# The first third of a turn: where two layer norms stand on VectorE and ScalarE

## The chip, the cores and the metric

The kernel runs on one core of one Trainium2 chip. The metric is the device time of that core in microseconds. Five engines work at once, each through its own instructions in order: TensorE (PE: products, and PEld: its weight loads), VectorE (DVE), ScalarE (ACT), GpSimd (POOL) and SyncE (SP), which here issues transfers. They wait for each other by semaphores.

## The reference, cut to what matters

The input is `x`, 64 graphs of 256 nodes with 256 features, and `adj`, 64 matrices of 256x256 with zeros and ones. Two layers follow each other, all in float32.

```python
# layer 0
h = _gat(x, adj, W1, a1);  h = _gat(h, adj, W2, a2)     # two graph attentions
h = _layernorm(x + h, g_ln1, b_ln1)                     # norm 0 in the kernel
ff = relu(h @ w_ff1 + b_ff1) @ w_ff2 + b_ff2
x = _layernorm(h + ff, g_ln2, b_ln2)                    # norm 1
# layer 1 (8 heads of 32)
scores = q @ k.T / sqrt(32);  attn = softmax(scores)
out = sum over r < 4 of (attn * (adj == r)) @ v_r
x = _ln(x + out @ Wo + bo, g1, beta1)                   # norm 2
ff = gelu(x @ W1 + b1) @ W2 + b2
return _ln(x + ff, g2, beta2)                           # norm 3
```

A norm is `(x - m) * rsqrt(v + eps) * g + b` with mean `m` and variance `v` over the 256 features of a node. With zeros and ones in `adj`, only two of the four values of `r` occur. A second path for other inputs is in the program; it doesn't run here.

## The kernel before, in words

**Groups and turns.** Two graphs make a group: 512 nodes, four blocks of 128. There are 32 groups, and the main loop calls `turn(y_, x_, z)` for u = 0 to 31 with three groups in three phases: `Y` (group u) goes through the attention and the hidden layer of layer 1, `X` (group u+1) through norm 0, the hidden layer of layer 0 and norm 1, and `Z` (group u+2) through the graph attentions. In turn 31 there is no `X`, in turns 30 and 31 no `Z`. The last norm (norm 3) of group u isn't done in its own turn: the turn puts `(y_, y)` on the list `waiting`, and the next turn does the norm in its first third. So turns 1 to 30 hold a waiting last norm and the first norm of `X`; turn 0 holds the first norm alone, turn 31 neither. The last two groups store their result piece by piece in another way.

**Order.** Inside `turn`, `tc.manual_schedule` makes the order of the text the order of TensorE, SP, VectorE and ScalarE (of TensorE and SP alone when there is no `X`). GpSimd's order is left to a scheduler.

**Products of seven.** The matrix products are done with seven products of quarters instead of eight. Their steps have numbers: `p("q1 v1 q2")` issues steps 1 of the query and key product (`q`), 1 of the value product (`v`) and 2 of `q`, each two matmuls in the source, four records in the trace. Two PSUM banks each collect them: steps 1, 6, 7, 4 go to one, steps 2, 5, 3 to the other. After 2, 5, 3 and 4 ScalarE copies the bank out (L1034), after 2, 6 and 7 VectorE adds (L1038). The next step into the same bank waits for that: v5 for the copy after v2, q7 for the sum after q6. The hidden layers do the same with `first("2a 1a 5a")`: a and b are two halves, ScalarE copies `h1b` (L905) after 2, 5 and 3, VectorE adds `h1a` (L908) after 1, 6 and 7.

**A norm** has these pieces. `moments`: one BN_STATS (L826) and one aggregation (L827) per block on VectorE. `norm`: the moments, then GpSimd's `rs = (v + eps) ** -0.5` (L837, L838). `applied_norm`: VectorE's offset `nm = -m * rs` (L846), then per block ScalarE's `y * rs + nm` (L853). The scale and shift of the last norm follow much later in the turn.

**The first third of a turn** in the order of the text: the four differences for the seven products (`p.sums()`); q1 v1 q2; norm 0 of `X` applied to blocks 0 and 1; the statistics of the waiting last norm, all four blocks; v2 q5; norm 0 applied to blocks 2 and 3, then `normed_features`, which transposes the four blocks on VectorE (L694) into `yt` and moves them into `hT` by 12 transfers on SP (L713) and four copies on GpSimd (L711); the scores of the first of four head groups (`sp`, L1082) and their exponentials (L1091), in two halves between v5, q3 and v3; the adjacency masks (`ea`, L1095); the waiting last norm applied, four blocks; the rest of the seven products; the sums over nodes (`es`, L1100). Then `first_hidden` forms four differences of `hT` (`tt`, L879), scores, masks and sums of the second head group follow, the early transpose of `Z`'s features (`xT`, L1137), and the hidden layer of `X` is dealt between the attention products: 2a 1a 5a, the scores of head group 2, the product with head group 1, 3a 6a, 2b 1b, and so on.

Of the kernel before, what the change touches and what calls it, by code (L numbers as in the profile page):

```python
# [12 lines left out]
ALU = mybir.AluOpType  # L13
# [372 lines left out]
def narrow_path(  # L386
# [13 lines left out]
    nc = tc.nc  # L400
# [6 lines left out]
    NB = N // P  # L407
# [281 lines left out]
    def normed_features(u, l, xn, natural=False, queues=(nc.sync,)):  # L689


        yt = work.tile([P, Q, KB, T, 32], F32, tag="yt", name=f"yt{u}_{l}", bufs=1)
        for t in range(T):
            mark["transposed"] = nc.vector.transpose(  # L694
                yt[:, :, :, t].rearrange("p q k r -> p k q r"),
                xn[:, t].rearrange("p (k q c) -> p k q c", k=KB, c=32))
        if natural:
            hT = work.tile([P, KB, TN], F32, tag="hT", name=f"hT{u}_{l}")
            to = hT.rearrange("c k (t a r) -> c (k t) a r", a=Q, r=32)
            for q in reversed(range(Q)):  # L700
                for a in range(Q):
                    move = nc.gpsimd.tensor_copy if q == a else nc.sync.dma_start
                    move(to[q * 32:(q + 1) * 32, :, a], yt[a * 32:(a + 1) * 32, q].rearrange("c k t r -> c (k t) r"))  # L703
            return with_ones([hT[:, k] for k in range(KB)])
        hT = work.tile([P, Q, KB, T, 32], F32, tag="hT", name=f"hT{u}_{l}")
        n = 0
        for q in range(Q):
            for a in range(Q):
                to, at = hT[q * 32:(q + 1) * 32, a], yt[a * 32:(a + 1) * 32, q]
                if q == a:  # L710
                    nc.gpsimd.tensor_copy(to, at)  # L711
                else:
                    mark["placed"] = queues[n % len(queues)].dma_start(to, at)  # L713
                    n += 1
        return [hT[:, :, k].rearrange("p a t r -> p t a r") for k in range(KB)]
# [100 lines left out]
    def normed(u, l, y, blocks=range(T)):  # L816

        applied_norm(y, *norm(u, l, y, blocks))

    def moments(u, l, y, blocks, mv=None):  # L820
        n = f"{u}_{l}_{blocks[0]}"
        st = work.tile([P, T, 6], F32, tag="st", name=f"st{n}", bufs=1)
        if mv is None:
            mv = work.tile([P, T, 2], F32, tag="mv", name=f"mv{n}")
        for t in blocks:
            nc.vector.bn_stats(st[:, t, :], y[:, t, :])  # L826
            nc.vector.bn_aggr(mv[:, t, :], st[:, t, :])  # L827
        return mv

    def norm(u, l, y, blocks=range(T), mv=None):  # L830

        n, t0 = f"{u}_{l}_{blocks[0]}", blocks[0]
        bt = slice(t0, t0 + len(blocks))
        mv = moments(u, l, y, blocks if mv is None else blocks[len(blocks) // 2:], mv)
        rs = work.tile([P, T], F32, tag="rs", name=f"rs{n}")
        nm = work.tile([P, T], F32, tag="nm", name=f"nm{n}")
        nc.gpsimd.tensor_scalar(rs[:, bt], mv[:, bt, 1], EPS, 0.0, op0=ALU.add, op1=ALU.add)  # L837
        nc.gpsimd.tensor_tensor(rs[:, bt], rs[:, bt], mhalf[:, bt], ALU.pow)  # L838
        if l == 3:
            nc.gpsimd.tensor_add(high[:, bt], high[:, bt], mv[:, bt, 0])  # L840
        return blocks, mv, rs, nm

    def applied_norm(y, blocks, mv, rs, nm, part=None, gpsimd=False):
        bt = slice(blocks[0], blocks[0] + len(blocks))
        if part is None or part[0] == blocks[0]:
            nc.vector.scalar_tensor_tensor(nm[:, bt], mv[:, bt, 0], -1.0, rs[:, bt],  # L846
                                           op0=ALU.mult, op1=ALU.mult)
        for t in part or blocks:
            if gpsimd:
                nc.gpsimd.tensor_scalar(y[:, t, :], y[:, t, :], rs[:, t:t + 1], nm[:, t:t + 1],  # L850
                                        op0=ALU.mult, op1=ALU.add)
                continue
            mark["normed"] = nc.scalar.activation(y[:, t, :], y[:, t, :], AF.Identity,  # L853
                                                  bias=nm[:, t:t + 1], scale=rs[:, t:t + 1])
# [145 lines left out]
    def out_sums(u, l):  # L1000
        two = [work.tile([P, HPB, NB * N], F32, tag=t, name=f"{t}q{u}_{l}") for t in ("e", "ea")]
        return [t[:, :, i * N:(i + 1) * N] for t in two for i in range(2)]
# [90 lines left out]
    def masked(b, m, ab, e, ea, pairs=(0, 2)):  # L1093
        for a in pairs:
            nc.vector.tensor_tensor(ea[:, a:a + 2, :], e[:, a:a + 2, :],  # L1095
                                    ab[:, None, :].to_broadcast([P, 2, NB * N]), ALU.mult)
# [112 lines left out]
    def first_hidden(x_):  # L1209

        X = g[x_]
        hT = X["hT"]
        if x_ == 0:
            hT = [h.rearrange("p (t a r) -> p t a r", t=T, r=32) for h in hT]
        X["h1"] = work.tile([P, FB, TN], F32, tag="h1", name=f"h1{x_}_0", bufs=1)
        tt = work.tile([P, Q, KB, T, 32], F32, tag="yt", name=f"tt{x_}_0", bufs=1)
        return hidden_seven(x_, 0, hT, wf1s, bf1, AF.Relu, X,
                            tt.rearrange("p q k t r -> p (q k t r)"))

    def piece():  # L1220
        if left:
            next(left[0], None)

    def turn(y_, x_, z):
        Y, X, Z = (g.get(u) for u in (y_, x_, z))
        hT, y = Y["hT"], Y["y"]
        quads = [(b, m) for b in range(G) for m in range(KB)]
        p = Projections(y_, hT)
# [5 lines left out]
        def scores(n, heads=range(HPB)):  # L1234
            pe[n], e[n] = weighted(y_, *quads[n], q, k_, Y["aT"])
            powers(n, heads)

        def powers(n, heads):
            exps(pe[n], *e[n], heads)

        def masks(n, *pairs):
            masked(*e[n], *pairs)

        def totals(n):
            e[n] = node_sums(*e[n])

        def sums(n):
            b, m = quads[n]
            if m == 0:
                acc[b] = [psum.tile([P, 512], F32, tag=t_, name=f"{t_}{y_}_{b}") for t_ in ("po", "zo")]  # L1250
            applied(b, m, v, *e.pop(n), *acc[b])
# [8 lines left out]
        def first(names, ends=0):  # L1260

            if X:
                steps(names)
            else:
                for _ in range(ends):
                    piece()
# [3 lines left out]
                                            ("PE", "SP", "DVE", "Activation")[:4 if X else 2]})  # L1270
        with order:
            p.sums()
            p("q1 v1 q2")
            if X:
                applied_norm(X["y"], *X["n"], [0, 1])
            last = norm(waiting[0][0], 3, waiting[0][1]) if waiting else None
            p("v2 q5")
            if X:
                applied_norm(X["y"], *X.pop("n"), [2, 3])
                X["hT"] = normed_features(x_, 0, X["y"])  # L1280
            scores(0, ())
            p("v5")
# [1 line left out]
            if z + 1 < NG:  # L1284
                load_x(z + 1)
            p("q3 v3")
            masks(0, (0,))
            powers(0, (2, 3))
            if waiting:
                applied_norm(waiting[0][1], *last)  # L1290
            p("q6 v6 q7 v7")
            masks(0, (2,))
            totals(0)
            p("q4 v4")
            steps = first_hidden(x_) if X else None
            scores(1)
            masks(1)
# [1 line left out]
            if Z:  # L1299
                early(z)  # L1300
            sums(0)
            first("2a 1a 5a", 1)
            scores(2)
            sums(1)
            if X:
# [32 lines left out]
            if Z:  # L1338
                mv = moments(y_, 2, y, range(NB))
            else:  # L1340
                n = norm(y_, 2, y, range(NB))
# [13 lines left out]
            if Z:  # L1355
                n = norm(y_, 2, y, mv=mv)
            else:
                applied_norm(y, *n)
                n = norm(y_, 2, y, range(NB, T))
# [41 lines left out]
            if X:  # L1401
                n = moments(x_, 1, X["y"], range(NB))
# [6 lines left out]
            if X:  # L1409
                out.add(4)  # L1410
                n = norm(x_, 1, X["y"], mv=n)
            h1 = Y["h1"] = work.tile([P, FB, TN], F32, tag="h1", name=f"h1{y_}_1", bufs=1)
            second("2a 1a 2b 1b")
            second("5a 5b")
            if X:
                applied_norm(X["y"], *n, [0])
            if Z:
                affine(y, rg3, rb3)
# [51 lines left out]
    waiting = []  # L1470

    with tc.manual_schedule(engines={mybir.EngineType.PE, mybir.EngineType.SP}):
# [24 lines left out]
        first = HiddenOut(0, 0, g[0]["y"], g[0]["h1"], wf2s, out_sums(0, 0))  # L1497
# [9 lines left out]
        for u in range(NG):  # L1507
            turn(u, u + 1, u + 2)
# [16 lines left out]
@with_exitstack  # L1525
def tile_gat_layer__then__relational_attention_layer(ctx: ExitStack, tc: tile.TileContext, *args):
    nc = tc.nc
    keep = ctx.enter_context(tc.tile_pool(name="keep", bufs=1))
    bad = keep.tile([1, 1], I32, name="bad")
    narrow_path(tc, *args, bad)  # L1530
    with tc.If(nc.values_load(bad[0:1, 0:1], min_val=0, max_val=P) > 0):
        general_path(tc, *args)
# [30 lines left out]
```

## Time and profile before

| what | us |
|---|---|
| median of three runs | 3070.12 (3069.05 to 3071.68) |
| the profiled execution | 3069.44 |
| its span in the trace | 3067.8 |
| TensorE busy | 3003.6 (98%) |
| VectorE busy | 2624.0 (86%) |
| ScalarE busy | 1684.2 (55%) |
| GpSimd busy | 678.4 (22%) |

The granted clock of TensorE was 0.995 of full speed. A line of a timeline gives the start in us, the time, the engine, the line of the kernel, the operation, what it writes and reads, the shape, how many records are merged in it, and in brackets the idle time of the engine ahead of it and what ended that. For merged records the time is that of the whole row.

### The profile page before, as it was taken

How to read it: one execution, taken by the hardware profiler on the slowest of the kernel's cores; microseconds unless marked ns; L12 is line 12 of the kernel's file. 1: busy time of each engine (PE TensorE's matmuls, PEld its weight loads, DVE VectorE, ACT ScalarE, POOL GpSimd, SP SyncE). 2: the span in 40 equal slices, each digit the busy share in tenths (PEclk: the TensorE clock that was granted, in tenths of full speed). 3: DMA queues.
4: the chain of work that ended last, by engine and by line, in shares of the span. 5: the costliest groups of instructions: out<-in, count | busy, mean ns of one | idle time of the engine just before them, and what ended most of it. 6: DMA issues, size and time to landing. Idle time of an engine off the chain costs nothing.

```text
span 3067.8 us, 58503 instructions
## 1 busy us (share of the span) xinstructions
PE 3003.6 (98%) x22192; PEld 2460.3 (80%) x22192; DVE 2624.0 (86%) x5025; ACT 1684.2 (55%) x3404; POOL 678.4 (22%) x930
## 2 busy tenths in 40 slices
PE   7999999999999999999999999999999999999997
PEld 5788877888887888787887778887878887878876
DVE  4788888888888889888888888888888888888886
ACT  4455555655645555555555455556555555555553
POOL 4222121222211221221222112222112212122211
PEclk8999999999999999999999999999999999999999
DMA  5011111211111211111111112111112111121000
GB/s 146 13 35 35 38 36 25 44 37 39 35 35 32 44 37 39 32 29 40 40 36 36 39 25 44 37 39 34 36 32 44 36 39 33 25 44 37 18 13 16
DMA packets 428403, 113.25 MB, mean 37 GB/s; under 512 B 364586, under 2 KB 427604, under 8 KB 428116
## 3 DMA queue, kind: packets, MB, share of 16 engines
q1 hardware_dynamic: 418076, 102.20, 15.2%
q10 hardware_dynamic: 8984, 6.19, 0.8%
q8 instruction: 178, 2.92, 0.4%
q0 software_dynamic: 1056, 1.05, 0.1%
q14 instruction: 109, 0.89, 0.1%
HBM read 56.78 MB, written 16.78 MB: 24 GB/s over the span
## 4 chain that ended last, share of the span: by engine, by line
PE 85%; DVE 9%; ACT 2%; issue 2%; DMA 1%; SPq 1%; POOL 1%; DVEq 0%; POOLq 0%; ACTq 0%
PE yf L985 22%; PE h1a L896 15%; PE h1b L896 11%; PE po L1110 7%; PE qk L1051 5%; PE v L1051 5%; PE xpp L740 4%; PE yop L811 4%; PE ygp L811 3%; PE sp L1082 3%; PE hpp L800 2%; PE zo L1113 2%; DVE s L775 2%; DVE yt L694 1%; DVE eaq L971 1%
## 5 line engine op out<-in xcount | busy, mean ns | idle before, releaser
L905 ACT COPY h<-h1b 128x512 f32<-128x512 f32 x384 | 224.2, 584 | 393.8 <-PE h1b L896 389.3
L908 DVE TENSOR_TENSOR h<-h1a,h 128x512 f32<-128x512 f32 x384 | 262.7, 685 | 111.9 <-PE h1a L896 106.2
L1095 DVE TENSOR_TENSOR ea<-e,aT 128x1024 f32<-128x1024 f32 x256 | 306.4, 1218 | 21.6 <-ACT e L1091 21.6
L853 ACT ACTIVATE y<-y,nm,rs 128x256 f32<-128x256 f32 x450 | 243.8, 607 | 140.1 <-DVE nm L846 135.8
L1091 ACT ACTIVATE e<-sp 128x512 f32<-128x512 f32 x512 | 269.4, 608 | 43.7 <-PE sp L1082 40.4
L1123 POOL TENSOR_TENSOR low<-low,rq 128x16 f32<-128x16 f32 x64 | 13.9, 217 | 1043.4 <-DVE rq L1122 1043.4
L1034 ACT COPY qk<-qk 128x512 f32<-128x512 f32 x128 | 75.3, 589 | 286.9 <-PE qk L1051 286.9
L711 POOL COPY hT<-yt 32x256 f32<-32x256 f32 x244 | 207.7, 851 | 68.4 <-DVE yt L694 60.8
L826 DVE BATCH_NORM_STATS2 st<-y 128x6 f32<-128x256 f32 x512 | 207.6, 407 | 4.5
L993 DVE TENSOR_TENSOR y<-yf,y 128x256 f32<-128x256 f32 x448 | 182.9, 408 | 29.5 <-PE yf L985 29.4
L837 POOL TENSOR_SCALAR rs<-mv 128x4 f32<-128x4 f32 (+1 forms) x134 | 33.1, 247 | 750.7 <-DVE mv L827 744.9
L865 DVE TENSOR_TENSOR y<-y,rb 128x1024 f32<-128x1024 f32 (+1 forms) x130 | 166.8, 1283 | 3.2
L939 ACT ACTIVATE h<-h,cols 128x512 f32<-128x512 f32 x256 | 167.0, 713 | 1.5 <-DVE h L908 1.1
L862 DVE TENSOR_TENSOR y<-y,rg 128x1024 f32<-128x1024 f32 (+1 forms) x130 | 161.6, 1243 | 1.2 <-ACT y L853 1.1
L1100 DVE TENSOR_TENSOR es<-e 128x1024 f32<-128x1024 f32 x128 | 155.6, 1216 | 0.0
L703 POOL COPY hT<-yt 32x256 f32<-32x256 f32 x120 | 114.8, 957 | 169.4 <-DVE yt L694 165.2
L838 POOL TENSOR_TENSOR rs<-rs,mhalf 128x4 f32<-128x4 f32 (+1 forms) x134 | 146.6, 1094 | 8.4
L1082 PE MATMUL sp<-qk 32*128 32x256 f32 x2048 | 146.6, 400 | 0.1
L742 ACT COPY xp<-xpp 128x260 f32<-128x260 f32 x128 | 45.4, 386 | 171.5 <-PE xpp L740 171.4
L1038 DVE TENSOR_TENSOR qk<-qk,qk 128x512 f32<-128x512 f32 x96 | 65.9, 686 | 83.9 <-ACT qk L1034 65.1
L1110 PE MATMUL po<-e,v 128*32 128x256 f32 x2048 | 136.3, 384 | 0.0
L896 PE MATMUL h1a<-tt,wf 128*128 128x256 f32 x512 | 134.2, 386 | 0.3 <-DVE h L908 0.3
(280 smaller groups left out, 7645.5 us busy)
## 6 DMA issues: line engine op xcount, KB each, us to landing
hT<-yt SPq DMA_DIRECT2D x912, 32.0 KB, 1.9
y<-in_x_dram SPq DMA_DIRECT2D x32, 512.0 KB, 4.5
xq<-in_x_dram SPq DMA_DIRECT2D x240, 64.0 KB, 2.2
aq<-in_adj_dram SPq DMA_DIRECT2D x240, 64.0 KB, 2.4
out_dram<-y SPq DMA_DIRECT2D x30, 512.0 KB, 2.9
hT<-yt ACTq DMA_DIRECT2D x180, 32.0 KB, 1.9
wf<-in_L_gnn_w_ff_dram SPq DMA_DIRECT2D x2, 1024.0 KB, 7.3
w<-in_L_gnn_W_dram SPq DMA_DIRECT2D x2, 1024.0 KB, 7.7
```

The lines of the kernel that those rows point to most:

```text
L711: nc.gpsimd.tensor_copy(to, at)
L811: nc.tensor.matmul(ps[:, i * F:(i + 1) * F], lhs(t, k), rhs(b, k), start=(k == 0), stop=(k == n - 1))
L853: mark["normed"] = nc.scalar.activation(y[:, t, :], y[:, t, :], AF.Identity, bias=nm[:, t:t + 1], scale=rs[:, t:t + 1])
L896: nc.tensor.matmul(ps[:, i * N:(i + 1) * N], w_[:, f * P:(f + 1) * P], m, start=first and i == 0, stop=True, skip_group_check=True)
L905: mark["copied"] = nc.scalar.copy(out(h, o, b), pair(ps))
L908: mark["added"] = nc.vector.tensor_tensor(out(h, o, b), pair(one[h]), out(h, o, b), ALU.add)
L985: nc.tensor.matmul(s.ps[n][:, i * F2:(i + 1) * F2], a[:, k, i * P:(i + 1) * P], w_[:, k, :], start=n in (1, 2, 5) and i == 0 and k == 0, s ...
L1051: nc.tensor.matmul(ps[:, i * N:(i + 1) * N], l, r, start=n in (1, 2, 5) and i == 0, stop=True, skip_group_check=True)
L1082: nc.tensor.matmul(ps[a][:, j * N:(j + 1) * N], k_[hp, m, j0:j0 + P], q[hp, m, b * N:(b + 1) * N], start=True, stop=True)
L1091: nc.scalar.activation(e[:, a, :], ps[a], AF.Exp, scale=isd)
L1095: nc.vector.tensor_tensor(ea[:, a:a + 2, :], e[:, a:a + 2, :], ab[:, None, :].to_broadcast([P, 2, NB * N]), ALU.mult)
L1110: nc.tensor.matmul(po[hp, m * N:(m + 1) * N], vs[:, hp], w[:, a, j * N:(j + 1) * N], start=(n == 0), stop=(n == len(terms) - 1))
```

## The change

The offset of a norm gets a function of its own, `offsets`, and `applied_norm` calls it only where it applies all blocks at once. For norm 0 of `X` the offset is issued ahead of q1, and the four applications are dealt out: block 0 after q2, block 1 after v2, blocks 2 and 3 after q5. The four transposes and the transfers stand where they stood, after block 3, but no statistics of the last norm stand ahead of v2 any more. These are split: two blocks after the second pair of exponentials and ahead of the first mask, two blocks after v4, with GpSimd's part of the norm behind them. The offset of the last norm and its first two applications come after steps 2a and 1a of the hidden layer, the other two after 5a. In the turn without an `X` the two halves of the first mask are issued together. Elsewhere `offsets` is called where `applied_norm` had formed the offset. No instruction is added or taken away; the order on TensorE and SP is the same; on GpSimd the four copies into `hT` now stand ahead of the last norm's three instructions.

```diff
--- before.py
+++ after.py
@@ -840,11 +840,13 @@
             nc.gpsimd.tensor_add(high[:, bt], high[:, bt], mv[:, bt, 0])
         return blocks, mv, rs, nm
 
+    def offsets(blocks, mv, rs, nm):
+        bt = slice(blocks[0], blocks[0] + len(blocks))
+        nc.vector.scalar_tensor_tensor(nm[:, bt], mv[:, bt, 0], -1.0, rs[:, bt], op0=ALU.mult, op1=ALU.mult)
+
     def applied_norm(y, blocks, mv, rs, nm, part=None, gpsimd=False):
-        bt = slice(blocks[0], blocks[0] + len(blocks))
-        if part is None or part[0] == blocks[0]:
-            nc.vector.scalar_tensor_tensor(nm[:, bt], mv[:, bt, 0], -1.0, rs[:, bt],
-                                           op0=ALU.mult, op1=ALU.mult)
+        if part is None:
+            offsets(blocks, mv, rs, nm)
         for t in part or blocks:
             if gpsimd:
                 nc.gpsimd.tensor_scalar(y[:, t, :], y[:, t, :], rs[:, t:t + 1], nm[:, t:t + 1],
@@ -1270,13 +1272,19 @@
                                             ("PE", "SP", "DVE", "Activation")[:4 if X else 2]})
         with order:
             p.sums()
+            if X:
+                n = X.pop("n")
+                offsets(*n)
             p("q1 v1 q2")
             if X:
-                applied_norm(X["y"], *X["n"], [0, 1])
-            last = norm(waiting[0][0], 3, waiting[0][1]) if waiting else None
-            p("v2 q5")
+                applied_norm(X["y"], *n, [0])
+            p("v2")
             if X:
-                applied_norm(X["y"], *X.pop("n"), [2, 3])
+                applied_norm(X["y"], *n, [1])
+            p("q5")
+            if X:
+                applied_norm(X["y"], *n, [2])
+                applied_norm(X["y"], *n, [3])
                 X["hT"] = normed_features(x_, 0, X["y"])
             scores(0, ())
             p("v5")
@@ -1284,14 +1292,18 @@
             if z + 1 < NG:
                 load_x(z + 1)
             p("q3 v3")
-            masks(0, (0,))
             powers(0, (2, 3))
             if waiting:
-                applied_norm(waiting[0][1], *last)
+                w, wy = waiting[0]
+                last = moments(w, 3, wy, range(NB))
+            if X:
+                masks(0, (0,))
             p("q6 v6 q7 v7")
-            masks(0, (2,))
+            masks(0, (2,) if X else (0, 2))
             totals(0)
             p("q4 v4")
+            if waiting:
+                last = norm(w, 3, wy, mv=last)
             steps = first_hidden(x_) if X else None
             scores(1)
             masks(1)
@@ -1299,7 +1311,14 @@
             if Z:
                 early(z)
             sums(0)
-            first("2a 1a 5a", 1)
+            if waiting:
+                first("2a 1a")
+                offsets(*last)
+                applied_norm(wy, *last, [0, 1])
+                first("5a")
+                applied_norm(wy, *last, [2, 3])
+            else:
+                first("2a 1a 5a", 1)
             scores(2)
             sums(1)
             if X:
@@ -1413,6 +1432,7 @@
             second("2a 1a 2b 1b")
             second("5a 5b")
             if X:
+                offsets(*n)
                 applied_norm(X["y"], *n, [0])
             if Z:
                 affine(y, rg3, rb3)
```

## Prediction

> **What bounds the kernel now.** I read the page first, then the gaps between turns, then one turn on each engine.
>
> Parts 1 and 4 of the page (busy time; the chain that ended last):
>
> ```profile
> PE 3003.6 (98%) x22192; PEld 2460.3 (80%) x22192; DVE 2624.0 (86%) x5025; ACT 1684.2 (55%) x3404; POOL 678.4 (22%) x930
> ...
> PE 85%; DVE 9%; ACT 2%; issue 2%; DMA 1%; SPq 1%; POOL 1%; DVEq 0%; POOLq 0%; ACTq 0%
> ```
>
> TensorE is the bound, and its program is the same in both kernels (so is SP's). So only TensorE's waits can change. By TensorE's timeline the first product of turn n starts 93.05 us after that of turn n-1 in most cases (93.05 to 94.57). A microsecond of waiting per turn is about 30 us, 1%.
>
> I take the turn that starts at 1040.08 and write r for time since then. TensorE's timeline shows 4 products of 128x256 taking 0.86 when nothing waits; where it takes more, something is late:
>
> ```profile
> 1044.57 1.15 PE L1082 MATMUL sp<-qk 32*128 32x256 f32 x16
> 1045.90 1.13 PE L1051 MATMUL v<-wvs,tq 128*128 128x256 f32 x4 [0.18 <-ACT v L1034]
> 1046.87 1.03 PE L1051 MATMUL qk<-hT,wqks 128*128 128x256 f32 x4
> 1047.85 1.13 PE L1051 MATMUL v<-wvs,hT 128*128 128x256 f32 x4
> ...
> 1050.96 1.13 PE L1051 MATMUL qk<-tq,wqk 128*128 128x256 f32 x4 [0.26 <-DVE qk L1038]
> ...
> 1064.42 1.13 PE L896 MATMUL h1b<-hT,wf1s 128*128 128x256 f32 x4
> ```
>
> These are sp, v5, q3, v3, q7 and, last, 3a of the hidden layer (r 24.34). v5 waits for ScalarE's v copy, q7 for VectorE's q6 sum. VectorE's timeline says why that sum is late, and where its queue is tight later:
>
> ```profile
> 1044.10 0.15 DVE L846 SCALAR_TENSOR_TENSOR nm<-mv,rs 128x4 f32<-128x4 f32 x1
> ...
> 1046.31 0.66 DVE L1038 TENSOR_TENSOR v<-v,v 128x512 f32<-128x512 f32 x1
> 1046.88 1.42 DVE L694 STREAM_TRANSPOSE yt<-y 128x256 f32<-128x256 f32 x4
> 1048.81 1.23 DVE L1095 TENSOR_TENSOR ea<-e,aT 128x1024 f32<-128x1024 f32 x1 [0.51 <-ACT e L1091]
> ...
> 1058.19 0.42 DVE L879 TENSOR_TENSOR tt<-hT 128x256 f32<-128x256 f32 x1 [2.24 <-DMA hT<-yt]
> ...
> 1063.07 1.23 DVE L1137 STREAM_TRANSPOSE xT<-xq 128x1024 f32<-128x1024 f32 x1
> 1064.23 0.65 DVE L908 TENSOR_TENSOR h<-h1a,h 128x512 f32<-128x512 f32 x1
> ```
>
> Between nm and the v sum stand four pairs of statistics (1044.17 to 1046.31). From the first tt to the h1a sum VectorE never rests: tt x4, ea x2, es, xT. ScalarE at that place has room and takes each hidden-layer copy as it comes:
>
> ```profile
> 1061.16 0.59 ACT L905 COPY h<-h1b 128x512 f32<-128x512 f32 x1 [1.22 <-PE h1b L896]
> 1062.27 2.07 ACT L1091 ACTIVATE e<-sp 128x512 f32<-128x512 f32 x4 [0.52 <-PE sp L1082]
> 1065.59 0.58 ACT L905 COPY h<-h1b 128x512 f32<-128x512 f32 x1 [1.26 <-PE h1b L896]
> ```
>
> **What the Trainium skill says.** "PSUM — Partial Sum Buffer", Engine vs sequencer instructions: the queues of ScalarE and VectorE are strict FIFO. The trace agrees: ScalarE's v copy, ready when v2 ended at about 1043.7, ran at 1045.29, after two normalisations that waited 0.83 for nm. "TensorE: Matmul & The Clock Gate", Part 2: weight loads are pulled ahead of running products, products keep their order. The trace agrees: a group whose weight load was held by a wait takes 0.97 instead of 0.86. "SBUF — State Buffer", Who interferes with whom: a VectorE operation with two SBUF inputs and a GpSimd read exclude each other. I charge nothing: ea beside GpSimd's four hT copies (1048.42 to 1051.17) took 1.23, later ones 1.22.
>
> **The change part by part.** TensorE waits are worked first; there are 30 turns with both a first norm and a waiting last norm (1 to 30), turn 0 has only the first.
>
> *First norm dealt out, offsets ahead.* nm needs GpSimd's rs, done at r 2.50, and VectorE is idle then (2.13 before the q sum), so nm is done at 2.7 for nothing. ScalarE, with a copy every 0.47 and a normalisation every 0.50: qk copy 2.80 as before, y0 3.27, v copy 3.77 to 4.33, y1 4.24, q5's copy 4.74, y2 5.21, y3 5.71 to 6.31. v5 no longer waits: it follows sp after 1.07 (5.57, was 5.82). q3 6.54, v3 7.37 (v copy 6.74 to 7.31; was 7.77), q6 8.34 (was 8.74).
>
> *Statistics off the v sum.* VectorE: q sum 3.41, v sum 4.37, transposes ending at y3 + 0.45 = 6.76 (was 8.22): 1.46 earlier. Two pairs of statistics (1.07) follow, until 7.85; hidden, because ea waits for the second exponential, ending 8.30. ea 8.34, q6 sum 9.48 (nm no longer between) to 10.17, q7 at 10.22, was 10.88. **Gain on TensorE: 0.66 a turn.** Only the 12 SP transfers and GpSimd's copies follow the transposes; they move 1.46 forward, no other SP work being ahead of them. GpSimd's rs of the last norm now comes after those copies, with 5 us to spare.
>
> *The other two pairs of statistics.* v7 is at 11.19; by the rows, v sum +1.07, ea +0.60, es +1.14, next +1.14: r 15.14. The two pairs take 1.09, so tt can't start before 16.23. In before tt starts when the last hT transfer lands: over the 30 turns r 17.31 to 19.51 (15 of them by 17.7), mean 17.95. After: the later of 16.23 and landing minus 1.46. The statistics thus lie in the old DMA gap (2.24 here).
>
> *Last norm applied inside the hidden layer.* Four activations go from an idle place (ScalarE waited 1.38 after them) to behind 2a's and 5a's copies, and the first waits for nm, which VectorE now issues only after 1a's sum. From tt to that sum is 6.04 in every turn with an xT. Then nm + 0.58, its time 0.15, ScalarE + 0.04, two activations 1.00, 5a's copy 0.57, TensorE + 0.05. So 3a = tt + 8.43. Behind the waiting activation on ScalarE stand 5a's copy (for which 3a waits), two more activations, four exponentials and all later hidden copies.
>
> With tt at 16.23, 3a is at 24.66. TensorE alone would be there at 24.33 - 0.66 = 23.67: **a new stall of about 1.0, which takes the gain and 0.33 more.** Where the transfer lands late, 3a = landing + 6.97: 25.1 for this turn's 18.11, was 24.34. Turn by turn over the 30 landings, and with turn 30 1.16 earlier (no xT), the mean of 3a goes from 24.51 to 25.00: 14.8 us in all.
>
> *What is late next.* With s the start of 5a's copy: activations s+0.47 and s+0.97, exponentials s+1.47 to about s+3.5, 3a's copy, then 2b's, ending s+4.48; 5b may load at s+4.54, that is 3a + 3.92. In before it is 3a + 3.56 (27.90 - 24.34). So 0.36 more a turn, 10.8 us. The 6a sum waits for 3a's late copy, and the products of 7 for such sums: the last, 7b, then loads at 3a + 8.55 against 8.19, the same 0.36, not a further one. From there VectorE and TensorE are shifted alike; nothing absorbs it, as TensorE is 98% busy.
>
> Sum: +14.8 + 10.8, less some 0.4 for turn 0 (v5's wait alone): **+25 us** on the profiled span of 3067.8 (its run 3069.44, the median of three 3070.12). On the median: **3095 us**.
>
> Bounds. The unknown term is when hT lands. If the transfers came no earlier at all, the same sum gives 3a at mean 26.34 and +66: 3136. If VectorE reached tt 0.6 sooner (15.6), +22; 0.7 later, +38. I take the shift of 1.46, since the transfers wait for the transposes and the SP queue is idle before them.
>
> **The rivals.**
> *nm is in time (faster).* Were nm done by r 22.0, 5a's copy would be no later than TensorE needs and the 0.66 would stay: 30 x 0.66 = 20 us, and some 4 us of the waits for landings: 3046. I have nm done at 23.0 at the earliest. The point of no change is 22.3 (3a at 23.97, with the 0.36 that follows). For it: only 0.7 separates 23.0 from 22.3. Against: the 6.04 is back to back work, not waits. Chance 0.11.
>
> *Gain and stall cancel (no change).* Early landings everywhere and a later burst that packs tighter than 0.36: within 6 us of 3070. Chance 0.07.
>
> *The hT landing doesn't follow the transposes, or ScalarE's burst reaches further (slower still).* Then 3115 to 3136. For it: landings scatter by 2.2 us for reasons the trace doesn't show. Against: each SP issue starts 0.14 after the last transpose in this turn. Chance 0.12.
>
> That the order isn't what the text says is excluded for VectorE and ScalarE where a turn has a first norm; the last turn's is unchanged.
>
> **How the numbers follow.** The forecast, 3095, has 0.70, with its own range 3076 to 3115 (from the scatter of landings and 0.5 us per turn either way). Slower 0.70 + 0.12 = 0.82, same 0.07, faster 0.11; 0.2% is about 6 us, what a measurement of this kernel can tell from no change. Leaving out the faster case and a little at either end gives 3072 to 3118.
>
> **What would show it.** Right: v5 1.07 after sp; q7 near r 10.2; transposes ending near 6.8; turns of 93.6 to 94.2 instead of 93.05; ScalarE's normalisations of the last norm waiting over 3 us for VectorE's nm; 3a's weight load waiting over 1 us for ScalarE; 5b 3.9 after 3a. Wrong: nm before r 22.3, or 3a without a wait, or turns under 93.

## The result and the profile after

The changed kernel took 3109.28 us in the median (3103.12 to 3112.01, four runs), the kernel before 3070.38 beside it: 1.0124 times as long, 95% interval 1.0106 to 1.0141. The profiled execution took 3103.12, its span 3101.5, 33.7 more than the span of before. It is the fastest of the four runs; a second trace of the changed kernel stands further down.

Parts 1 and 4 of the page of the changed kernel:

```profile
PE 3009.4 (97%) x22192; PEld 2460.4 (79%) x22192; DVE 2642.4 (85%) x5025; ACT 1678.8 (54%) x3404; POOL 652.8 (21%) x930
...
PE 73%; DVE 14%; ACT 7%; issue 2%; SPq 2%; DMA 1%; POOL 1%; DVEq 0%; POOLq 0%; ACTq 0%
```

No engine works more, but the chain that ended last runs less through TensorE (85% before) and more through VectorE (9% before) and ScalarE (2%). TensorE's timeline of the turn that starts at 1050.73 (r is again the time since a turn's start), the one that answers to the turn at 1040.08:

```profile
1056.29 1.13 PE L1053 MATMUL v<-wvs,tq 128*128 128x256 f32 x4
...
1061.06 1.13 PE L1053 MATMUL qk<-tq,wqk 128*128 128x256 f32 x4
...
1073.97 0.61 PE L1115 MATMUL zo<-es,ones 128*32 128x256 f32 x8
1076.44 1.13 PE L898 MATMUL h1b<-hT,wf1s 128*128 128x256 f32 x4 [1.85 <-ACT h L907]
```

v5 comes at r 5.56 (5.82 before), q7 at 10.33 (10.88), 3a at 25.71 (24.34), after a wait of 1.85 for ScalarE's copy of h1b. VectorE in the same turn:

```profile
1053.26 0.16 DVE L845 SCALAR_TENSOR_TENSOR nm<-mv,rs 128x4 f32<-128x4 f32 x1 [1.25 <-POOL rs L838]
1054.14 0.69 DVE L1040 TENSOR_TENSOR qk<-qk,qk 128x512 f32<-128x512 f32 x1 [0.72 <-ACT qk L1036]
1055.11 0.69 DVE L1040 TENSOR_TENSOR v<-v,v 128x512 f32<-128x512 f32 x1 [0.28 <-ACT v L1036]
1055.72 1.80 DVE L694 STREAM_TRANSPOSE yt<-y 128x256 f32<-128x256 f32 x4
...
1068.03 0.43 DVE L881 TENSOR_TENSOR tt<-hT 128x256 f32<-128x256 f32 x1 [0.90 <-DMA hT<-yt]
...
1074.08 0.65 DVE L910 TENSOR_TENSOR h<-h1a,h 128x512 f32<-128x512 f32 x1
1074.65 0.14 DVE L845 SCALAR_TENSOR_TENSOR nm<-mv,rs 128x4 f32<-128x4 f32 x1
```

The transposes end at r 6.79 instead of 8.22. The first tt to 1a's sum is 6.05, and nm follows it. ScalarE waits for exactly that:

```profile
1069.44 0.59 ACT L907 COPY h<-h1b 128x512 f32<-128x512 f32 x1 [1.31 <-PE h1b L898]
1074.83 1.09 ACT L855 ACTIVATE y<-y,nm,rs 128x256 f32<-128x256 f32 x2 [4.80 <-DVE nm L845]
1075.82 0.56 ACT L907 COPY h<-h1b 128x512 f32<-128x512 f32 x1
1076.29 1.09 ACT L855 ACTIVATE y<-y,nm,rs 128x256 f32<-128x256 f32 x2
1077.28 2.03 ACT L1093 ACTIVATE e<-sp 128x512 f32<-128x512 f32 x4
```

It stands idle for 4.80 with 5a's copy behind the waiting activation; the copy is ready to run at 1071.2, when 5a ends, and runs at 1075.82. A common turn starts 94.15 after the one before it, instead of 93.05.

### The profile page after: what moved, and what is told of

It is laid out like the page before. It is cut to its first block, busy times and chain, and to the rows that moved or that the text cites. A ratio compares the mean times of both kernels' runs of the same rounds, so it can differ in the third digit from the quotient of the medians.

```text
span 3101.5 us, 58413 instructions
## 1 busy us (share of the span) xinstructions
PE 3009.4 (97%) x22192; PEld 2460.4 (79%) x22192; DVE 2642.4 (85%) x5025; ACT 1678.8 (54%) x3404; POOL 652.8 (21%) x930
## 3 DMA queue, kind: packets, MB, share of 16 engines
q8 instruction: 178, 2.92, 0.4%
## 4 chain that ended last, share of the span: by engine, by line
PE 73%; DVE 14%; ACT 7%; issue 2%; SPq 2%; DMA 1%; POOL 1%; DVEq 0%; POOLq 0%; ACTq 0%
PE yf L987 22%; PE h1a L898 13%; PE h1b L898 8%; PE po L1112 5%; PE qk L1053 4%; PE xpp L740 4%; PE v L1053 4%; PE yop L811 4%; PE ygp L811 3%; PE sp L1084 3%; ACT e L1093 3%; DVE ea L1097 2%; ACT y L855 2%; PE hpp L800 2%; DVE s L775 2%
## 5 line engine op out<-in xcount | busy, mean ns | idle before, releaser
L1093 ACT ACTIVATE e<-sp 128x512 f32<-128x512 f32 x512 | 269.0, 606 | 23.1 <-PE sp L1084 19.5
L711 POOL COPY hT<-yt 32x256 f32<-32x256 f32 x244 | 177.1, 726 | 184.9 <-DVE yt L694 172.7
L703 POOL COPY hT<-yt 32x256 f32<-32x256 f32 x120 | 114.7, 956 | 170.0 <-DVE yt L694 165.8
L694 DVE STREAM_TRANSPOSE yt<-y 128x256 f32<-128x256 f32 x364 | 136.0, 417 | 4.7 <-ACT y L855 0.3
L1112 PE MATMUL po<-ea,v 128*32 128x256 f32 x2048 | 134.3, 379 | 0.0
```

Source lines behind the costliest of these rows:

```text
L1093: nc.scalar.activation(e[:, a, :], ps[a], AF.Exp, scale=isd)
L1112: nc.tensor.matmul(po[hp, m * N:(m + 1) * N], vs[:, hp], w[:, a, j * N:(j + 1) * N], start=(n == 0), stop=(n == len(terms) - 1))
```

## The experiments

The theory: the loss is the wait of the last norm's activations for nm, in ScalarE's queue ahead of 5a's copy, and a smaller one behind it, because the same queue holds two more activations ahead of the exponentials. Rivals: VectorE is held up by the two late pairs of statistics ahead of tt; the four activations cost ScalarE time where the hidden layer needs it; the first norm's part is what costs. All edits are to the changed kernel.

### nm formed earlier

```diff
             scores(1)
+            if waiting:
+                offsets(*last)
             masks(1)
...
                 first("2a 1a")
-                offsets(*last)
                 applied_norm(wy, *last, [0, 1])
```

> The changed kernel, but the last norm's offset nm is formed ahead of the second head group's masks, some 5 us earlier on VectorE; its four activations stay between the hidden layer's copies on ScalarE. If the wait of those activations for nm makes the loss, 3a no longer waits, a turn takes about 92.5 us instead of 94.15 (93.05 in the kernel before), and the time is about 3050, 20 us under the kernel before. If the two pairs of statistics ahead of tt, or the four activations' own time among the hidden copies, make the loss, nothing changes: 3103 to 3112.

Measured: 3050.34 (3048.95 to 3051.60) against 3071.88 for the kernel before, ratio 0.9933 (0.9916 to 0.9950). A common turn takes 92.51. ScalarE's timeline in a common turn:

```profile
1144.89 0.58 ACT L907 COPY h<-h1b 128x512 f32<-128x512 f32 x1 [1.31 <-PE h1b L898]
1145.38 1.09 ACT L855 ACTIVATE y<-y,nm,rs 128x256 f32<-128x256 f32 x2
1146.70 0.58 ACT L907 COPY h<-h1b 128x512 f32<-128x512 f32 x1 [0.23 <-PE h1b L898]
1147.18 1.09 ACT L855 ACTIVATE y<-y,nm,rs 128x256 f32<-128x256 f32 x2
1148.18 2.04 ACT L1093 ACTIVATE e<-sp 128x512 f32<-128x512 f32 x4
```

The same instructions in the same ScalarE order, without the wait: 5a's copy now waits only for TensorE, and 3a comes at r 23.79, 3.37 after the scores of head group 2, as in the kernel before. The statistics stand where they stood and the activations too, so neither costs anything of its own once nm is early. (What the statistics cost by way of a late nm this run doesn't tell; the account of the prediction comes back to it.) This kernel beats both others.

### nm one instruction earlier

```diff
             sums(0)
             if waiting:
+                offsets(*last)
+            if waiting:
                 first("2a 1a")
-                offsets(*last)
                 applied_norm(wy, *last, [0, 1])
```

> The changed kernel with nm one VectorE instruction earlier, ahead of 1a's sum instead of behind it. If 3a hangs on nm, 3a and the turn come 0.58 us earlier in 30 turns: 17 us under the changed kernel, about 3091. If VectorE's load or the statistics make the loss, the same as the changed kernel.

Measured: 3087.61 (3086.78 to 3088.10), ratio to before 1.0053 (1.0037 to 1.0070): 15.7 above the kernel before, where the changed one is 39 above (37 when it was run again). In the trace 3a of a common turn is at 24.47 instead of 25.07, 0.60 earlier, and the turn is as much shorter: it follows nm one to one. The traced spans differ by 16.4 (3085.0 against 3101.5), close to the 17 expected; the medians differ by 21.7, because the untraced runs of the changed kernel were slower than its first traced one.

### VectorE's work ahead of nm made longer, with nm late and with nm early

```diff
         nc.vector.transpose(xT.rearrange("p k n -> p (k n)"), d["xq"].rearrange("p k n -> p (k n)"))
+        nc.vector.transpose(xT.rearrange("p k n -> p (k n)"), d["xq"].rearrange("p k n -> p (k n)"))
```

In the changed kernel:

> The changed kernel with the early transpose of the features issued twice into the same tile: one more VectorE instruction of 1.2 us (start to start 1.16) ahead of 1a's sum and nm, in the 29 turns after the first that have it; the result is the same. If the turn hangs on nm, 3a comes 1.16 us later (26.2 after the turn's start in a common turn) and the time is some 34 us above the changed kernel, about 3142. If VectorE's work at this place is hidden, the same as the changed kernel.

In the kernel with nm formed earlier:

> The same second transpose in the kernel with nm formed early. 1a's sum comes 1.16 us later, at about 23.9 in a common turn, ending 24.6, and 6a waits for it from 24.6 on: nearly hidden. About 3050 to 3055 against 3050 without the second transpose, so that the 34 us of the other kernel are the wait for nm and not VectorE's work. If VectorE's work as such is on the path, some 34 us more here too, about 3084.

Measured: 3155.49 (3152.86 to 3156.89), ratio 1.0271 (1.0254 to 1.0289), against 3056.92 (3056.10 to 3059.64), ratio 0.9955 (0.9938 to 0.9972). The same transpose costs some 46 us ahead of a late nm and 6.6 us behind an early one (3056.92 less 3050.34), a little more than expected. So VectorE's work here is nearly hidden; what isn't is the wait behind it.

The 46 is more than the 34 expected. 1a's sum came 1.28 later, not 1.16 (r 23.98 against 22.70), which is 37 in 29 turns. The rest is something I hadn't expected. In 11 of the 30 turns 5b came over 4.5 after 3a instead of 3.89. TensorE's timeline and, below it, the table of stretches (busy time of PE, PEld, DVE, ACT, POOL with counts, then TensorE's granted clock, the transfers' share and GB/s) of such a turn:

```profile
1084.04 0.61 PE L1115 MATMUL zo<-es,ones 128*32 128x256 f32 x8
1087.77 1.13 PE L898 MATMUL h1b<-hT,wf1s 128*128 128x256 f32 x4 [3.12 <-ACT h L907]
1088.74 1.46 PE L898 MATMUL h1a<-tt,wf1s 128*128 128x256 f32 x4
1089.99 1.91 PE L898 MATMUL h1b<-hT,wf 128*128 128x256 f32 x4
1091.69 1.49 PE L898 MATMUL h1a<-hT,wf 128*128 128x256 f32 x4
1093.02 1.03 PE L898 MATMUL h1b<-tt,wf1s 128*128 128x256 f32 x4
```

```profile
1084.00:1087.00 3.00, 0.65 (x13) 0.13 (x4) 2.93 (x6) 0.84 (x2) 0.00 (x0) 1.00 0.13 20
1087.00:1090.00 3.00, 2.23 (x9) 1.90 (x10) 1.44 (x3) 3.00 (x7) 0.22 (x1) 0.87 0.77 123
1090.00:1093.00 3.00, 3.00 (x9) 2.43 (x8) 1.82 (x2) 1.71 (x4) 0.00 (x0) 0.56 0.25 38
1093.00:1096.00 3.00, 3.00 (x15) 2.48 (x14) 2.42 (x3) 0.70 (x2) 0.00 (x0) 1.00 0.00 0
```

After the wait TensorE is granted 0.87 and then 0.56 of its clock; the same four matmuls take up to 1.91 instead of 1.03. Over the 11 turns 5b is late by 15.9 in all, and 37 + 15.9 is the 53 by which this span (3154.4) exceeds the changed kernel's first one.

### TensorE's wait filled with products

To see whether idleness lowers the clock, the small products of head group 1 with ones are issued four times, to the same result, in the kernel with two transposes and nm late:

```diff
-        for a in range(HPB):
+        for a in list(range(HPB)) * (4 if waiting and (b, m) == (0, 1) else 1):
             nc.tensor.matmul(zo[a * DH:(a + 1) * DH, m * N:(m + 1) * N], ones, es[:, a, :],
```

> The kernel with the second transpose ahead of nm (3155), in which 11 of 30 turns show TensorE at a lower granted clock just after its wait ahead of 3a; here the four small products with ones ahead of that wait (zo of head group 1) are issued four times over, to the same result, so that TensorE works through 1.65 us of the some 2.6 us of waiting. If idleness itself lowers the clock, those turns are gone, 3a stays at 26.35 in a common turn, and the time falls to about 3140. If the clock falls for another reason (the transfers of that stretch, the lateness), some ten turns show it still, and the time stays at 3155.

Measured: 3142.16 (3139.58 to 3142.61), 13.3 under the kernel without the extra products. 3a is at 26.35 in a common turn as before, and such turns are 2 of 30 instead of 11 (2.7 us in place of 15.9). In only four turns did TensorE still wait 2.06 to 2.10 ahead of 3a, in the others at most 1.53, and the two are among the four. The mean clock of all four runs was 0.994 or 0.995, against 0.988 to 0.990 without the extra products. More products made the kernel faster:

```profile
1084.24 1.91 PE L1115 MATMUL zo<-es,ones 128*32 128x256 f32 x32
1087.35 1.13 PE L898 MATMUL h1b<-hT,wf1s 128*128 128x256 f32 x4 [1.20 <-ACT h L907]
1088.31 1.03 PE L898 MATMUL h1a<-tt,wf1s 128*128 128x256 f32 x4
```

### The changed kernel once more

> The changed kernel once more, for a trace of another execution: the recorded one took 3103.1, the other three 3108.5 to 3112.0 at a mean clock lower by 0.001 to 0.002. If turns of lowered clock make that difference, a trace of a run above 3106 shows some of them (5b more than 4.5 us after 3a), which the first trace doesn't; if late transfers make it, it shows a larger mean of 3a without such turns.

Measured: 3108.82 (3106.98 to 3109.41), ratio 1.0120 (1.0103 to 1.0137). The traced execution took 3108.68, span 3107.0. It has three turns of lowered clock (4.1 us), the first trace none; the mean of 3a is 25.31 against 25.22 (2.7 us in 30 turns). Together 6.8, against a difference of spans of 5.5: both were at work.

### The last two activations later

```diff
                 first("5a")
-                applied_norm(wy, *last, [2, 3])
...
             first("2b 1b")
+            if waiting:
+                applied_norm(wy, *last, [2, 3])
```

> The changed kernel with the last two activations of the last norm behind 2b's copy instead of ahead of the exponentials of head group 2. If they are what makes 5b wait 0.36 us more than 3a does, 5b is back at 3a + 3.6, and the time is some 11 us under the changed kernel, about 3097. If the 0.36 comes from elsewhere, the same as the changed kernel.

Measured: 3092.52 (3091.40 to 3095.01), ratio 1.0068 (1.0051 to 1.0084). In a common turn 3a stays at 25.07 and 5b comes 3.56 after it instead of 3.89. The traced span, 3093.4, is 8.1 under the changed kernel's first (which had no turn of lowered clock, this one has one of 1.4), so the 0.33 of 30 turns, 10, is there. The medians differ by more, 16.8; turns of lowered clock in the untraced runs would explain it, which isn't shown.

### Each half of the change alone

The first norm alone (statistics, offset and application of the last norm as before):

```diff
             if X:
                 applied_norm(X["y"], *n, [0])
+            last = norm(waiting[0][0], 3, waiting[0][1]) if waiting else None
             p("v2")
...
+            masks(0, (0,))
             powers(0, (2, 3))
             if waiting:
-                w, wy = waiting[0]
-                last = moments(w, 3, wy, range(NB))
-            if X:
-                masks(0, (0,))
+                applied_norm(waiting[0][1], *last)
...
-            if waiting:
-                first("2a 1a")
-                offsets(*last)
-                applied_norm(wy, *last, [0, 1])
-                first("5a")
-                applied_norm(wy, *last, [2, 3])
-            else:
-                first("2a 1a 5a", 1)
+            first("2a 1a 5a", 1)
```

> Only the first norm's part of the change: its offset ahead of the products and its four applications dealt between the copies; statistics, offset and application of the last norm as before. v5 is free (5.57 after the turn's start), q7 comes at about 10.6 instead of 10.88, since nm of the last norm still stands ahead of the q6 sum; transposes no earlier than before. About 0.27 us a turn: 3062, 8 us under the kernel before.

Measured: 3066.67 (3063.44 to 3070.19, 20 runs), ratio 0.9984 (0.9978 to 0.9991). v5 at 5.57, q7 at 10.66, a common turn 92.83: 0.22 saved rather than 0.27, and 5 us in all.

The last norm alone (the first norm's offset and pairs as before):

```diff
+            p("q1 v1 q2")
             if X:
                 n = X.pop("n")
                 offsets(*n)
-            p("q1 v1 q2")
-            if X:
-                applied_norm(X["y"], *n, [0])
-            p("v2")
-            if X:
-                applied_norm(X["y"], *n, [1])
-            p("q5")
+                applied_norm(X["y"], *n, [0, 1])
+            p("v2 q5")
             if X:
-                applied_norm(X["y"], *n, [2])
-                applied_norm(X["y"], *n, [3])
+                applied_norm(X["y"], *n, [2, 3])
```

> Only the last norm's part of the change: its statistics split and later, its offset behind 1a's sum, its activations between the hidden layer's copies; the first norm applied in two pairs as before. v5 waits as before (5.82 after the turn's start); transposes end near 7.7 instead of 6.8 or 8.2; tt no sooner than about 17.0, 3a at 25.4. A common turn takes about 94.5: some 10 us above the changed kernel, 3112 to 3120.

Measured: 3133.69 (3127.02 to 3140.42), ratio 1.0204 (1.0184 to 1.0224). The shortest turns take 94.45 to 94.5 as expected, but the time is above the expectation: tt waits for hT in most turns and starts as late as r 19.1 (17.6 in the mean, against 16.8 in the changed kernel), which now moves 3a one to one, and five turns had the lowered clock (6.8 us). The parts don't add up, 62 - 5 against 39 for both: the first half brings hT forward, and the second half is what hangs on it.

## Why the prediction was right

The direction and the mechanism held: v5, the transposes, the wait of the activations, the length of a turn and 5b behind 3a all came as named. 3109 lies in the forecast's own range, 3076 to 3115, but near its upper end: 25 was forecast, against 34 by the traced spans and 39 by the medians. Of the 34, the later 3a and the burst behind it make 32 (21.5 and 10.5, below); the 5 more of the medians are, by the second trace, turns of lowered clock and later landings.

- **The dealt first norm.** v5 as worked (5.57), q6 8.34, transposes' end 6.76 worked and 6.79 measured. q7 was 10.33 instead of 10.22, since ea took 1.33 here and not 1.23, so the gain was 0.55, not 0.66. The prediction charged nothing for ea and GpSimd's copies side by side, as ea had taken 1.23 beside them; in the kernel before it was a copy that was held up (last section), now it is ea.
- **hT follows the transposes.** Right; that rival is out. By the transfers' semaphore events the last one landed at r 17.65 in the mean of the 30 turns before and at 16.20 after: 1.45 earlier, where 1.46 was worked. In the changed kernel tt starts as early as 16.5 and as late as 17.9, where before it was 17.3 to 19.5.
- **The floor of tt.** Mis-sized: worked as 16.23, measured 16.62 in the common turn. 0.11 came with q7, and VectorE idles 0.22 between the last aggregation and tt, which before lay inside the wait for the transfers and didn't show. The mean of 3a was therefore 25.22 instead of 25.00 (24.51 before): 21.5 us, not 15. This is the term of the sum that was mis-sized most.
- **3a = tt + 8.43.** Measured 8.45 (25.07 less 16.62). Moving nm alone (3087.6, 3050.3) shows that 3a hangs on nm. The statistics count by way of it: in 19 of the 30 turns tt follows them after 0.22, though hT had landed 0.2 to 1.1 before. Had tt started 0.30 after each landing, its mean lag in the kernel before, it would come at 16.50 in the mean instead of 16.83, so they hold some 10 of the 34 us. This is an estimate from the traces; no run took the statistics away with nm late.
- **The burst behind it.** 0.36 worked, 0.33 measured at 5b, 0.35 at the next scores (r 34.67 less 25.07 against 33.58 less 24.33); the shift of two activations removed it at 5b.
- **Turn 0.** A gain of 0.4 was worked in; the first trace shows turn 1 starting 1.0 later than before (201.9 against 200.8). Turn 0 itself took 97.91 against 98.02; what came later is its start, 103.96 against 102.81, ahead of which the text of both kernels is the same. Over the eleven traces it lies anywhere between 102.8 and 104.4, for reasons left open.
- **What was not foreseen:** the lowered clock after a wait of over 2 us. The first trace of the changed kernel has none of it, the second 4.1 us.
- **The faster rival** failed where I had put its threshold, by about 1 us: nm was done at 23.4 in the common turn, 22.3 was needed, and one VectorE instruction earlier (0.60) was still not enough; ahead of five, it was.

## What to carry to other kernels

Where a queue is strictly in order, an instruction moved into an idle stretch brings its wait with it: price it by when its input is ready at the new place, and count what stands behind it on that engine. Form small inputs such as nm as soon as their own inputs are ready, not next to their use; here the 0.15 us instruction cost 59 us by standing behind 5 us of other VectorE work (3109 against 3050). And a change that frees one engine early can be worth having even when the whole is slower: look which half lost before undoing both. Here the first half alone gave 5 us (3066.67), and the second with nm early 16 more (3050.34).

## What the runs showed of the hardware that was not expected

**A wait of 2 us can cost TensorE its clock.** By the traces, the next products ran slower after some waits and not after others of the same length. Taking as the stall how much 3a is later than 3.37 after the scores of head group 2: in the traces of the changed kernel and of those that move nm, the last two activations or one half of the change, no turn with a stall under 2.05 showed it; of the 21 with 2.05 to 2.25, 9 did; of the 29 with 2.5 to 3.5 in the kernel with two transposes and nm late, 11. In a kernel without a second wait behind it, 5b came 5.24 after 3a instead of 3.56: 1.68 lost. That idleness is the cause is shown by the filled wait (2 turns instead of 11).

The Trainium skill, "TensorE: Matmul & The Clock Gate", Part 1, tells of a free-running window of about 3.4 us and of half the clock after an idle one. The clock records in the traces agree on the window and the half. From the start of turn 1 to that of turn 31 the granted clock is 1 or 0.5; the eleven traces hold 22 half-speed stretches there, 21 of 3.41 us and one of twice that, and within a trace all begin on one grid of 3.41. But the window need not be idle. In the 22 grid windows just ahead of these stretches TensorE was busy for 0.17 to 0.42 of the time; in every one of the some 9000 others it was busy for 0.43 or more. So about 2.0 us of idleness (0.58 of 3.41) were enough, if they fell into one window. Two turns of the changed kernel's second trace, both with a wait of 2.10 ahead of 3a, in stretches laid on the grid (columns as above):

```profile
1072.17:1075.58 3.41, 1.80 (x36) 0.81 (x28) 3.34 (x7) 1.11 (x3) 0.15 (x1) 1.00 0.17 28
1075.58:1079.00 3.42, 2.92 (x14) 2.59 (x15) 1.20 (x2) 3.42 (x8) 0.06 (x1) 1.00 0.70 110
1263.32:1266.73 3.41, 1.31 (x11) 0.99 (x6) 2.96 (x7) 2.70 (x6) 0.22 (x1) 1.00 0.51 81
1266.73:1270.14 3.41, 3.41 (x10) 2.70 (x9) 1.12 (x2) 2.26 (x6) 0.00 (x0) 0.50 0.49 78
```

The first wait is cut by a window's end, so TensorE is busy for 1.80 of the one window and 2.92 of the next, and its clock stays. The second falls into one window, with 1.31 busy, and the next window runs at 0.50. This line at 0.42 to 0.43 was read from the traces afterwards; no run was made to test it. Before turn 1, where TensorE has other work as well, it doesn't hold: in the changed kernel's first trace a window that was busy for 0.95 was followed by half speed too.

**GpSimd's copies and VectorE's mask.** In the kernel before, four GpSimd copies of hT that overlap the first ea take 2.75 together; in the changed one, where they come mostly ahead of it, 1.70. The difference is one copy: the second starts just after ea and takes 1.45 instead of 0.39, ending 0.26 after ea does. The ea that took 1.33 instead of 1.23 started while the last copy ran. The Trainium skill, "SBUF — State Buffer", Who interferes with whom, says that a VectorE instruction with two SBUF inputs contends with a GpSimd instruction that reads SBUF, and that the order of issue decides who blocks; the traces agree, as each time it is the one that starts second that takes longer. This is read from the traces; no run tested it.
